# Beginning the linear attention's preparation earlier in a fused attention, expert and linear-attention kernel

## The chip, the core and the metric

The kernel runs on one core of one Trainium2 chip. The time is device microseconds of that core, the median of repeated executions; before the change it is 2023.33 us (three runs, 2021.16 to 2025.43). The core has TensorE (PE: matrix products and transposes), VectorE (DVE), ScalarE (ACT), GpSimd (POOL) and SyncE (SP, which issues most transfers). Each engine takes its own instructions strictly in the order in which the program writes them, and waits on semaphores for the others. "PEld" in the profile is TensorE's loading of weights.

## What is computed

Four layers on x of 4 batches x 1024 tokens x 128 features, all in float32, each with a layer norm before and a residual sum after:

```python
x = L0_attn_a_x
x = x + _L0_attn_a_ref(_layernorm(x, axis=-1), ...)   # causal softmax attention, 16 heads of 64
x = x + _L0_ffn_ref(_layernorm(x, axis=-1), ...)      # 32 experts, the best 2 for each token
x = x + _L0_attn_b_ref(_layernorm(x, axis=-1), ...)   # gated linear attention, 16 heads of 8
x = x + _L0_ffn_ref(_layernorm(x, axis=-1), ...)      # the same experts again
```

The linear attention is causal over the tokens of a batch and works on features of the projections:

```python
qf = softplus(q) * (g + 1e-6);  kf = softplus(k)          # g = sigmoid(x @ Wg.T + bg)
kv_cum = cumsum(kf[..., :, None] * v[..., None, :], axis=2);  z_cum = cumsum(kf, axis=2)
out = einsum('bhtd,bhtde->bhte', qf, kv_cum) / (einsum('bhtd,bhtd->bht', qf, z_cum) + 1e-6)[..., None]
out = out.transpose(0, 2, 1, 3).reshape(B, T, h * dh) @ Wo.T
```

## The kernel before

x stays in on-chip memory throughout, as 32 tiles of 128 tokens x 128 features (`x_sb`); batch b has the tiles 8b to 8b+7. The order of the instructions is written out by hand: helpers are generators, and each `next()` puts one more piece of a helper into the program. What is named "turn" or "slot" below is a place in this written order, not a time.

**Attention** (lines 477 to 834). For each batch and each of 8 pairs of heads, `project` computes qT and kT (the pieces pk and pq) and the values va (two pieces pv of 8 records each in the profile), and eight `slot`s work on one block of 128 rows each: scores `s` (L588), maxima `nmx` (L597), exponentials `p`, sums, transposes `pt` (L677) and the weighted values `po` (L694). The pieces of the next pair are put between the slots. For the very first pair all six pieces of `project(0, 0)` stand ahead of the first slot. Every second pair, `project_out` adds the output projection `pw` (L709) to x (L714 on DVE). For the batches 0 to 2 the experts run beside the next batch's attention by sorting (`experts`: scatter to memory, 128-row products, and 16 gathering transfers L439 that POOL issues and that add into x). What of batch 2's gathers isn't issued when attention ends stands in `queue` and is issued later.

After the last slot, `project_out` for the last pairs of batch 3 is written as a loop over 8 tiles, with the layer-norm statistics of four tiles after each fourth (`statistics`, L122 to L127, whose `rstd_mf` comes from POOL). Then SP loads all 32 expert matrices, `we_sb`, in four parts (L844) into memory that held, among other things, `wo_sb`.

**Dense experts for batch 3** ("f", lines 1115 to 1145). The last eight tiles are two groups of four (`qs`). `routed` makes the weights of the experts for a group: normalized x (`xn_f`, L873, DVE), transposes and copy (`xnT_f`, L885, ACT), router logits `pl_f` (L892), softmax (`ex_f`, L905, ACT), the best two (`w_f`, L925, DVE). `dense` then takes a pair of tiles at a time, in eight steps g of four experts: one product `pe_f` of 128x512 for each tile (L956; five PSUM banks), whose four quarters are weighted and summed. In five of the steps DVE does this straight into x (L978, 8 instructions); in the steps 1, 4 and 6 ACT writes the weighted quarters to buffers `t_f` (L966) and POOL sums them: L972 for two buffers, then the halvings L990 and L991. This sum, the tile's share, is added to x by DVE (L937) in `settle`: two pairs later at the first step of a pair, and for the last two pairs by `settle(0)`, at the end of `dense`.

Beside the dense experts stand the first two preparations of the linear attention, `prepare(0)` and `prepare(1)`, each for four tiles of batch 0: statistics (L1024, L1025 on DVE, a chain of four small operations L1030 to L1033 on POOL), normalized x (`xn_l`, L1039, ACT), transposes and copy (`xnT_l`), four projections `pj` (L1057) with four copies each on ACT, exponential, sigmoid and logarithm on ACT, `y` (L1079, DVE), four sums on POOL (L1086, L1087) and a product on DVE (L1092). The pieces are placed by two rules. While the first `routed` is written, each of its 15 pieces is followed by one piece of `prepare(0)`. Then `fill(turn)` runs in each of 64 turns of `dense`: one piece of one preparation, each fourth turn one entry of `queue`, and in turn 56 the product `products(0)`, that is `kv(0)` (L1100, POOL).

**Linear attention** (lines 1147 to 1248). For each of the 32 tiles u: PE adds `kv(u)` into running sums in PSUM (`cum`, L1162), POOL makes `kv(u+1)`, DVE multiplies the sums with q (`m`, L1182), PE adds the rest that the next tile needs (`carry`, L1170, which has to wait for `m`), DVE finishes (`num`, L1191, and three small operations), and later pieces transpose, project and add to x. `ahead` puts pieces of the preparations 2 to 7 between these. The sums of a POOL product and those of the dense experts stand in one queue, POOL's.

**The experts again** ("s", lines 1250 to 1272): batch 0 by sorting, beside the dense form for the batches 1 to 3, with 18 buffers of the pool `mps`.

The names that the steps below use: `project` and the loop over `pairs` (L721 to L824), the `project_out` loop (L830), `routed` (L851), `dense` and `settle` (L928 to L995), `prepare` (L1018), `products` (L1095), `fill` (L1122), and the loop over u (L1228).

Of the kernel before, what the change touches and what calls it, by code (L numbers as in the profile page):

```python
# [8 lines left out]
F32 = mybir.dt.float32  # L9
U32 = mybir.dt.uint32  # L10
AF = mybir.ActivationFunctionType
# [4 lines left out]
P = 128  # L16
# [4 lines left out]
def hybrid_kernel(  # L21
# [450 lines left out]
        nc.sync.dma_start(out=out_v[b], in_=x_sb[:, c0 : c0 + NB, :])  # L472


    sides, queue = [], []
    banks = [None]
    with attn as ph:

        ph.enter_context(tc.manual_schedule())
# [240 lines left out]
        EARLY = (1, 5)  # L720
        for _ in normed(0):  # L721
            pass
        cur, ahead = project(0, 0)
        for _ in ahead:
            pass
        units = []
        weighing = []
        outs, norms = iter(()), iter(())
# [66 lines left out]
        for i, (b, pr) in enumerate(pairs):  # L795
            nm = f"{b}_{pr}"
            qT, kT, va = cur
            oT = otp.tile([P, N], F32, tag="oT", name=f"oT_{nm}")
            oTs.append(oT)
            ahead = iter(())  # L800
            if pr == NPAIR - 3 and b + 1 < B:
                norms = normed(b + 1)
            if i + 1 < len(pairs):
                nxt, ahead = project(*pairs[i + 1])
            twos = {}
            for k, ib in enumerate(ORDER):
# [12 lines left out]
                slot(u, (nm, ib - 1, twos[two], va, oT), k)  # L819
            if i + 1 < len(pairs):  # L820
                cur = nxt
            if pr % HALF == HALF - 1:
                pend = (b, range(pr + 1 - HALF, pr + 1), oTs)
                oTs = []  # L824
# [6 lines left out]
        for c, _ in enumerate(project_out(*pend)):  # L831
            if c % 4 == 3:
                c0 = (B - 1) * NB + c - 3
                known.append(statistics(c0, 4, f"mf_{c0 // 4}"))

    tc.no_sync_barrier()

# [90 lines left out]
    def dense(nm_, qs, store, pool, mp, ps_e, known, beside):  # L928
# [16 lines left out]
        for i, q in enumerate(qs):  # L945
# [46 lines left out]
                    due.append((x_sb[:, q * 4 + c, :], s, q * 4 if c == 3 else None))  # L992
            for _ in nxt:
                pass
        settle(0)  # L995

    lin = ExitStack()
    lw = lin.enter_context(tc.tile_pool(name="lw", bufs=1, reuse_waits="tile"))
    lb = lin.enter_context(tc.tile_pool(name="lb", bufs=3, reuse_waits="tile"))
    lp = lin.enter_context(tc.tile_pool(name="lp", bufs=3, reuse_waits="tile"))
    G = 4
    NE = LD + 1
    PARTS = 3
    EP = NE // PARTS

    tri, eps = mtri, epsn[:, :G]
# [4 lines left out]
    feats = {}  # L1016

    def prepare(t, pool):  # L1018

        c0 = t * G  # L1020
        st = small.tile([P, G, nc.vector.BN_STATS_DIM], F32, tag="stl", bufs=2, name=f"st_l{t}")
        mv = small.tile([P, G, nc.vector.BN_AGGR_DIM], F32, tag="mvl", bufs=2, name=f"mv_l{t}")
        for c in range(G):
            nc.vector.bn_stats(st[:, c, :], x_sb[:, c0 + c, :])  # L1024
            nc.vector.bn_aggr(mv[:, c, :], st[:, c, :])  # L1025
            if c == 1:
                yield
        rstd = small.tile([P, G], F32, tag="rstdl", bufs=2, name=f"rstd_l{t}")
        nb = small.tile([P, G], F32, tag="nbl", bufs=2, name=f"nb_l{t}")
        nc.gpsimd.tensor_tensor(rstd, mv[:, :, 1], eps, ALU.add)  # L1030
        nc.gpsimd.tensor_tensor(rstd, rstd, mhalf[:, :G], ALU.pow)
        nc.gpsimd.tensor_tensor(nb, mv[:, :, 0], rstd, ALU.mult)
        nc.gpsimd.tensor_scalar(nb, nb, -1.0, None, ALU.mult)  # L1033
        yield
        yield
        xn = lb.tile([P, G, D], F32, tag="xn", bufs=2, name=f"xn_l{t}")
        xnT = lb.tile([P, G * P], F32, tag="xnT", bufs=2, name=f"xnT_l{t}")
        for c in range(G):
            nc.scalar.activation(  # L1039
                xn[:, c, :], x_sb[:, c0 + c, :], AF.Identity,  # L1040
                scale=rstd[:, c : c + 1], bias=nb[:, c : c + 1],
            )
        yield
        pt = pool.tile([P, 512], F32, tag="ps1", name=f"pxn_l{t}")
        for c in range(G):
            nc.tensor.transpose(pt[:, c * P : (c + 1) * P], xn[:, c, :], ident)
        nc.scalar.copy(xnT, pt)
        yield
        kq = lb.tile([P, G, 2 * P], F32, tag="kq", name=f"kq_{t}")
        y = lb.tile([P, G, 2 * P], F32, tag="y", bufs=2, name=f"y_{t}")  # L1050
        u = lb.tile([P, G, 2 * P], F32, tag="u", bufs=2, name=f"u_{t}")
        ln = lb.tile([P, G, 2 * P], F32, tag="ln", bufs=2, name=f"ln_{t}")
        gt = lb.tile([P, G, P], F32, tag="gt", bufs=2, name=f"gt_{t}")
        va = lb.tile([P, G, P], F32, tag="va", name=f"va_{t}")
        for c in range(G):
            pj = pool.tile([P, 512], F32, tag="ps1", name=f"pj_{t}_{c}")
            nc.tensor.matmul(  # L1057
                pj, xnT[:, c * P : (c + 1) * P], wc.rearrange("p w d -> p (w d)"),
                start=True, stop=True,
            )  # L1060
            nc.scalar.activation(y[:, c, :], pj[:, : 2 * P], AF.Abs)
            nc.scalar.activation(kq[:, c, :], pj[:, : 2 * P], AF.Relu)
            nc.scalar.copy(gt[:, c, :], pj[:, 2 * P : 3 * P])
            nc.scalar.copy(va[:, c, :], pj[:, 3 * P :])
            if c == G - 1:
                nc.gpsimd.tensor_tensor(
                    gt, gt, bg_sb.unsqueeze(1).to_broadcast([P, G, P]), ALU.add
                )
            yield


        nc.scalar.activation(y, y, AF.Exp, scale=-1.0)
        nc.scalar.activation(u, y, AF.Copy, bias=1.0)
        yield
        yield
        nc.scalar.activation(gt, gt, AF.Sigmoid)
        yield
        yield
        nc.vector.scalar_tensor_tensor(y, u, 1.0, y, ALU.subtract, ALU.subtract)  # L1079
        nc.scalar.activation(ln, u, AF.Ln)  # L1080
        yield
        yield
        yield
        for i in range(2):
            cols = slice(i * P, (i + 1) * P)
            nc.gpsimd.tensor_tensor(ln[:, :, cols], ln[:, :, cols], y[:, :, cols], ALU.subtract)  # L1086
            nc.gpsimd.tensor_tensor(kq[:, :, cols], kq[:, :, cols], ln[:, :, cols], ALU.add)  # L1087
            yield
        yield
        yield  # L1090
        q = kq[:, :, P:]
        nc.vector.scalar_tensor_tensor(q, gt, 1e-6, q, ALU.add, ALU.mult)  # L1092
        feats[t] = (kq, va)

    def products(u):  # L1095

# [16 lines left out]
                sides.remove(e)  # L1113

    with ExitStack() as ph:
        mp = ph.enter_context(tc.tile_pool(name="mpf", bufs=12, reuse_waits="tile"))
        ps_f = ph.enter_context(tc.tile_pool(name="ps_f", bufs=3, space=PSUM, reuse_waits="tile"))
        ps_e = ph.enter_context(tc.tile_pool(name="ps_ef", bufs=5, space=PSUM, reuse_waits="tile"))
        banks[0] = ps_f
        preps = [prepare(t, ps_f) for t in range(2)]  # L1120

        def fill(turn):  # L1122

            if turn == 56:
                for p in preps:
                    for _ in p:
                        pass
                feats["kv"] = products(0)
            next(preps[turn % 2], None)
            if turn % 4 == 3:  # L1130
                if queue:
                    queue.pop(0)()
                on()

        qs = list(range(NT // 4 - 2, NT // 4))
        for _ in routed(qs[0], f"f_{qs[0]}", ps_f, known[0]):
            next(preps[0], None)
        dense("f", qs, False, ps_f, mp, ps_e, known, fill)
        for p in preps:
            for _ in p:  # L1140
                pass
        while sides or queue:
            if queue:
                queue.pop(0)()
            on()

    with lin as ph:
# [80 lines left out]
        for u in range(NT + 4):  # L1228
# [9 lines left out]
            if u < NT:  # L1238
# [24 lines left out]
    with ExitStack() as ph:  # L1263
# [41 lines left out]
```

## Time and profile before

| | |
|---|---|
| median of three runs | 2023.33 us |
| the profiled execution | 2022.32 us |
| its span, first to last instruction | 2020.6 us |
| busy PE, DVE, ACT, POOL | 1887.1, 1500.4, 1228.5, 1136.2 us |
| attention, to the last output projection | 0 to about 1474 us |
| output projection, first router weights | 1474 to 1503 us |
| dense experts of batch 3 | 1503 to 1572 us |
| change to linear attention | 1572 to 1592 us |
| linear attention | 1592 to 1777 us |
| the experts again | 1777 to 2021 us |

A line of the timeline has start, length, engine, line of the program, operation, result and operands, and in brackets how long the engine had stood idle before and what ended that. A line with "x2" merges two instructions that follow each other. A product in float32 with 128x512 results shows as two records. Shares of busy time over the whole span say little here, since the stages have different limits; the busy time by stage and the waits in it say more.

### The profile page before, as it was taken

Reading aid. Unit: us, or ns where it says so; the run is one execution under the profiler, and the core shown is the slowest. Engines: PE = TensorE matmul, PEld = TensorE weight load, DVE = VectorE, ACT = ScalarE, POOL = GpSimd, SP = SyncE. Lnnn points to the kernel's source line nnn. Section 1 sums busy time; section 2 is a strip of 40 time slices with the busy share of each in tenths; the row PEclk is TensorE's granted clock in tenths of the full one; section 3 lists DMA queues with packets and bytes.
Section 4 is the critical chain, followed back from the end, with each engine's and each line's share of the span. In section 5 each row is a group of like instructions: output and inputs, shape, how many; then the busy total and the mean of one; then the engine's idle time right before and its main releaser. Section 6 shows DMA issues by size and latency. Waiting matters only on the chain.

```text
span 2020.6 us, 33597 instructions
## 1 busy us (share of the span) xinstructions
PE 1887.1 (93%) x10066; PEld 1052.0 (52%) x10066; DVE 1500.4 (74%) x4467; ACT 1228.5 (61%) x3889; POOL 1136.2 (56%) x2080
## 2 busy tenths in 40 slices
PE   6999999999999999999999999999979788888897
PEld 3555555555555655555565555555643344543453
DVE  5776776776787676778867776776748778978877
ACT  4766666766667566766766676676645466344433
POOL 3444444454666466556834954665438666537737
PEclk9999999999999999999999999999989899988999
DMA  7000000000002310000132100003311000000251
GB/s 215 1 1 1 1 1 1 1 1 1 1 12 79 108 21 12 1 1 1 45 107 57 21 1 1 1 13 93 101 45 13 6 0 1 0 1 12 62 147 47
DMA packets 111875, 62.54 MB, mean 31 GB/s; under 512 B 5552, under 2 KB 110160, under 8 KB 111568
## 3 DMA queue, kind: packets, MB, share of 16 engines
q1 hardware_dynamic: 101936, 50.43, 8.8%
q0 software_dynamic: 9472, 8.40, 2.1%
q8 instruction: 82, 1.34, 0.3%
q10 hardware_dynamic: 288, 1.57, 0.2%
q14 instruction: 97, 0.79, 0.1%
HBM read 35.60 MB, written 24.77 MB: 30 GB/s over the span
## 4 chain that ended last, share of the span: by engine, by line
PE 63%; DVE 17%; ACT 10%; POOL 7%; issue 3%; DMA 1%; SPq 0%; ACTq 0%; POOLq 0%; DVEq 0%
PE s L588 19%; PE po L694 10%; PE pt L677 10%; DVE nmx L597 5%; PE pe_s L956 4%; ACT p L622 4%; PE pw L709 3%; PE pk L537 3%; DVE x_sb L978 3%; ACT pT L681 2%; PE pe L417 2%; PE pv L551 2%; ACT p L627 1%; PE cum L1162 1%; PE cum L1170 1%
## 5 line engine op out<-in xcount | busy, mean ns | idle before, releaser
L597 DVE TENSOR_REDUCE nmx<-s 128x2 f32<-128x1024 f32 x512 | 604.5, 1220 | 214.5 <-PE s L588 206.2
L622 ACT ACTIVATE p<-s,nmx 128x512 f32<-128x512 f32 (+3 forms) x640 | 360.8, 575 | 309.6 <-DVE nmx L597 277.5
L588 PE MATMUL s<-kT,qT 64*128 64x512 f32 x2048 | 517.8, 619 | 7.8 <-ACT p L622 4.5
L664 POOL TENSOR_SCALAR p<-p,f,ri 128x512 f32<-128x512 f32 (+3 forms) x768 | 502.5, 670 | 0.9 <-issue 0.6
L677 PEld LDWEIGHTS pt<-ident,p 128*128 128x128 f32 x2304 | 250.0, 141 | 218.0 <-issue 90.4
L677 PE MATMUL pt<-ident,p 128*128 128x128 f32 x2304 | 336.0, 282 | 23.4 <-POOL rs L642 7.1
L681 ACT COPY pT<-pt 128x512 f32<-128x512 f32 (+3 forms) x768 | 324.1, 509 | 14.8 <-PE pt L677 10.4
L646 POOL TENSOR_TENSOR rs<-rs,f 128x2 f32<-128x2 f32 x256 | 51.8, 202 | 437.2 <-ACT f L613 407.7
L694 PE MATMUL po<-pT,va 128*64 128x256 f32 (+1 forms) x2560 | 291.1, 365 | 0.6 <-DVE oT L701 0.6
L588 PEld LDWEIGHTS s<-kT,qT 64*128 64x128 f32 x2048 | 173.1, 185 | 195.2 <-issue 95.0
L627 ACT ACTIVATE p<-s,nmx 128x128 f32<-128x128 f32 x512 | 180.3, 365 | 107.5 <-DVE nmx L597 104.8
L694 PEld LDWEIGHTS po<-pT,va 128*64 128x64 f32 x2560 | 167.0, 136 | 97.2 <-issue 32.6
L956 PE MATMUL pe_s<-we_sb,xnT_s 128*128 128x512 f32 x384 | 184.9, 630 | 9.2 <-ACT t_s L966 5.5
L978 DVE SCALAR_TENSOR_TENSOR x_sb<-pe_s,w_s,x_sb 128x128 f32<-128x128 f32 x480 | 129.8, 341 | 32.7 <-PE pe_s L956 31.3
L635 DVE SCALAR_TENSOR_TENSOR p<-p,qtri 128x128 f32<-128x128 f32 x512 | 145.3, 311 | 7.0 <-ACT p L627 3.7
L642 POOL TENSOR_TENSOR rs<-rs 128x2 f32<-128x2 f32 x192 | 43.8, 228 | 187.4 <-DVE ri L655 187.4
L622 ACT ACTIVATION_READ_ACCUMULATOR p<-s,nmx 128x1 f32 x640 | 138.9, 217 | 0.0
L956 PEld LDWEIGHTS pe_s<-we_sb,xnT_s 128*128 128x128 f32 x384 | 74.0, 202 | 100.2 <-issue 58.4
L966 ACT ACTIVATE t_s<-pe_s,w_s 128x128 f32<-128x128 f32 x288 | 78.4, 380 | 50.2 <-PE pe_s L956 47.1
L714 DVE TENSOR_TENSOR x_sb<-pw,x_sb 128x128 f32<-128x128 f32 x128 | 36.9, 289 | 79.5 <-PE pw L709 79.1
L972 POOL TENSOR_TENSOR t_s<-t_s,t_s 128x512 f32<-128x512 f32 x48 | 60.2, 1272 | 60.8 <-ACT t_s L966 60.1
L709 PE MATMUL pw<-wo_sb,oT 128*128 128x128 f32 x512 | 84.5, 290 | 1.8 <-DVE x_sb L714 1.0
(302 smaller groups left out, 2677.0 us busy)
## 6 DMA issues: line engine op xcount, KB each, us to landing
xs<-xs_d SPq DMA_DIRECT2D x33, 256.0 KB, 3.0
ys_d<-ys SPq DMA_DIRECT2D x33, 256.0 KB, 2.4
we<-_ffn_expert_weights_dram SPq DMA_DIRECT2D x24, 256.0 KB, 3.8
xs_d<-zero SPq DMA_DIRECT2D x2, 3008.0 KB, 18.4
we<-_ffn_expert_weights_dram SPq DMA_DIRECT2D x45, 64.0 KB, 1.8
xs_s<-xs_d SPq DMA_DIRECT2D x11, 256.0 KB, 3.7
ys_d<-ys_s SPq DMA_DIRECT2D x11, 256.0 KB, 2.8
we_sb<-_ffn_expert_weights_dram SPq DMA_DIRECT2D x4, 512.0 KB, 6.1
```

Source lines behind the costliest of these rows:

```text
L588: nc.tensor.matmul(st[:, h, :], self.qT[rows, self.ib * P : (self.ib + 1) * P], self.kT[rows, j * 512 : (j + 1) * 512], start=True, stop=True,
L597: nc.vector.tensor_reduce(self.nmx[:, i, :], self.s[i], AX.X, ALU.max, negate=True)
L622: nc.scalar.activation(self.p[h][:, at : at + m * P], self.s[i][:, h, : m * P], AF.Exp, bias=bias, accum_out=self.rs[:, i, h : h + 1],)
L627: nc.scalar.activation(self.p[h][:, at + m * P : at + (m + 1) * P], self.s[i][:, h, m * P : (m + 1) * P], AF.Exp, bias=bias,)
L635: nc.vector.scalar_tensor_tensor(d, d, 1.0, qtri, ALU.mult, ALU.mult, accum_out=self.rs[:, 2, h : h + 1])
L664: nc.gpsimd.tensor_scalar(w, w, self.f[:, i, h : h + 1], self.ri[:, h : h + 1], ALU.mult, ALU.mult,)
L677: nc.tensor.transpose(pt[:, c * P : (c + 1) * P], self.p[h][:, (g + c) * P : (g + c + 1) * P], ident,)
L681: nc.scalar.copy(self.pTs[h][:, g : g + m, self.col : self.col + P], pt[:, : m * P].rearrange("p (c i) -> p c i", c=m),)
L694: nc.tensor.matmul(po[h * DH : (h + 1) * DH, c0:256], va[:, jb, h, :], pTs[h][:, jb, c0:], start=(jb == 0), stop=(jb == n - 1),)
L709: nc.tensor.matmul(pw[:, :P], oTs[i][:, c * P : (c + 1) * P], wo_sb[:, pr, :], start=(i == 0), stop=(i == len(prs) - 1),)
L956: nc.tensor.matmul(pe, xnT[:, c * P : (c + 1) * P], we_sb[:, 4 * g : 4 * g + 4, :].rearrange("p e d -> p (e d)"), start=True, stop=True,)
L978: nc.vector.scalar_tensor_tensor(xs, pe[:, e * D : (e + 1) * D], w[:, c, 4 * g + e : 4 * g + e + 1], xs, ALU.mult, ALU.add,)
```

## The change

- The first two preparations begin in the loop of the last output projection: after the tiles 0, 1, 2 one piece of `prepare(0)` each, after 4, 5, 6 one of `prepare(1)`. That covers the statistics and POOL's four operations; the third piece of each is empty.
- While the first `routed` is written, only eight of its pieces are followed by one of `prepare(0)`: `xn_l` at its first, the transposes at the fifth, the projections only after the router's logits have been written.
- In `fill`, `queue` is served each third turn and `products(0)` comes in turn 46.
- `dense` no longer ends with `settle(0)` but returns `settle`. For batch 3 it is called in the linear attention, after tile u = 1's `finish` has begun; for the last stage at once. For this the buffers `mpf` are reserved outside the linear attention's and kept through it, and these lie 24 KB further up in each partition.
- Of `project(0, 0)` four pieces (kT and qT) stand ahead of the first slot; the two pv pieces come one after each of the first two slots.

The body of `prepare` is moved up unchanged, with a small class `Bank` that hands it the pool of the moment.

```diff
+    class Bank:
+        def tile(self, *a, **k):
+            return banks[0].tile(*a, **k)
+
+    preps = [prepare(t, Bank()) for t in range(2)]
...
-        cur, ahead = project(0, 0)
-        for _ in ahead:
-            pass
+        cur, rest_ = project(0, 0)
+        for _ in range(4):
+            next(rest_)
...
                 slot(u, (nm, ib - 1, twos[two], va, oT), k)
+                next(rest_, None)
...
                 known.append(statistics(c0, 4, f"mf_{c0 // 4}"))
+            elif c < 7:
+                next(preps[c // 4])
...
-        settle(0)
+        return settle
...
+    shares = ExitStack()
+    mpf = shares.enter_context(tc.tile_pool(name="mpf", bufs=12, reuse_waits="tile"))
...
-        preps = [prepare(t, ps_f) for t in range(2)]
...
-            if turn == 56:
+            if turn == 46:
...
-            if turn % 4 == 3:
+            if turn % 3 == 2:
                 if queue:
                     queue.pop(0)()
...
-        for _ in routed(qs[0], f"f_{qs[0]}", ps_f, known[0]):
-            next(preps[0], None)
-        dense("f", qs, False, ps_f, mp, ps_e, known, fill)
+        for i, _ in enumerate(routed(qs[0], f"f_{qs[0]}", ps_f, known[0])):
+            if i in (0, 4, 8, 9, 10, 11, 12, 13):
+                next(preps[0])
+        settle = dense("f", qs, False, ps_f, mpf, ps_e, known, fill)
...
             ahead(3 * u + 2)
+            if u == 1:
+                settle(0)
...
+    shares.close()
...
-        dense("s", qs, True, ps_s, mp, ps_e, [None] * len(qs), pieces)
+        dense("s", qs, True, ps_s, mp, ps_e, [None] * len(qs), pieces)(0)
```

More of the change, by code (lines that the diff above doesn't have):

```diff
@@ L472, in experts, with prepare @@
         nc.sync.dma_start(out=out_v[b], in_=x_sb[:, c0 : c0 + NB, :])
+    G = 4
+    tri, eps = mtri, epsn[:, :G]
+    feats = {}
+    def prepare(t, pool):
+        c0 = t * G
+        st = small.tile([P, G, nc.vector.BN_STATS_DIM], F32, tag="stl", bufs=2, name=f"st_l{t}")
+        mv = small.tile([P, G, nc.vector.BN_AGGR_DIM], F32, tag="mvl", bufs=2, name=f"mv_l{t}")
+        for c in range(G):
+            nc.vector.bn_stats(st[:, c, :], x_sb[:, c0 + c, :])
+            nc.vector.bn_aggr(mv[:, c, :], st[:, c, :])
+            if c == 1:
+                yield
+        rstd = small.tile([P, G], F32, tag="rstdl", bufs=2, name=f"rstd_l{t}")
+        nb = small.tile([P, G], F32, tag="nbl", bufs=2, name=f"nb_l{t}")
+        nc.gpsimd.tensor_tensor(rstd, mv[:, :, 1], eps, ALU.add)
+        nc.gpsimd.tensor_tensor(rstd, rstd, mhalf[:, :G], ALU.pow)
+        nc.gpsimd.tensor_tensor(nb, mv[:, :, 0], rstd, ALU.mult)
+        nc.gpsimd.tensor_scalar(nb, nb, -1.0, None, ALU.mult)
+        yield
+        yield
+        xn = lb.tile([P, G, D], F32, tag="xn", bufs=2, name=f"xn_l{t}")
+        xnT = lb.tile([P, G * P], F32, tag="xnT", bufs=2, name=f"xnT_l{t}")
+        for c in range(G):
+            nc.scalar.activation(
+                xn[:, c, :], x_sb[:, c0 + c, :], AF.Identity,
+                scale=rstd[:, c : c + 1], bias=nb[:, c : c + 1],
+            )
+        yield
+        pt = pool.tile([P, 512], F32, tag="ps1", name=f"pxn_l{t}")
+        for c in range(G):
+            nc.tensor.transpose(pt[:, c * P : (c + 1) * P], xn[:, c, :], ident)
+        nc.scalar.copy(xnT, pt)
+        yield
+        kq = lb.tile([P, G, 2 * P], F32, tag="kq", name=f"kq_{t}")
+        y = lb.tile([P, G, 2 * P], F32, tag="y", bufs=2, name=f"y_{t}")
+        u = lb.tile([P, G, 2 * P], F32, tag="u", bufs=2, name=f"u_{t}")
+        ln = lb.tile([P, G, 2 * P], F32, tag="ln", bufs=2, name=f"ln_{t}")
+        gt = lb.tile([P, G, P], F32, tag="gt", bufs=2, name=f"gt_{t}")
+        va = lb.tile([P, G, P], F32, tag="va", name=f"va_{t}")
+        for c in range(G):
+            pj = pool.tile([P, 512], F32, tag="ps1", name=f"pj_{t}_{c}")
+            nc.tensor.matmul(
+                pj, xnT[:, c * P : (c + 1) * P], wc.rearrange("p w d -> p (w d)"),
+                start=True, stop=True,
+            )
+            nc.scalar.activation(y[:, c, :], pj[:, : 2 * P], AF.Abs)
+            nc.scalar.activation(kq[:, c, :], pj[:, : 2 * P], AF.Relu)
+            nc.scalar.copy(gt[:, c, :], pj[:, 2 * P : 3 * P])
+            nc.scalar.copy(va[:, c, :], pj[:, 3 * P :])
+            if c == G - 1:
+                nc.gpsimd.tensor_tensor(
+                    gt, gt, bg_sb.unsqueeze(1).to_broadcast([P, G, P]), ALU.add
+                )
+            yield
+        nc.scalar.activation(y, y, AF.Exp, scale=-1.0)
+        nc.scalar.activation(u, y, AF.Copy, bias=1.0)
+        yield
+        yield
+        nc.scalar.activation(gt, gt, AF.Sigmoid)
+        yield
+        yield
+        nc.vector.scalar_tensor_tensor(y, u, 1.0, y, ALU.subtract, ALU.subtract)
+        nc.scalar.activation(ln, u, AF.Ln)
+        yield
+        yield
+        yield
+        for i in range(2):
+            cols = slice(i * P, (i + 1) * P)
+            nc.gpsimd.tensor_tensor(ln[:, :, cols], ln[:, :, cols], y[:, :, cols], ALU.subtract)
+            nc.gpsimd.tensor_tensor(kq[:, :, cols], kq[:, :, cols], ln[:, :, cols], ALU.add)
+            yield
+        yield
+        yield
+        q = kq[:, :, P:]
+        nc.vector.scalar_tensor_tensor(q, gt, 1e-6, q, ALU.add, ALU.mult)
+        feats[t] = (kq, va)
@@ L1005, in hybrid_kernel @@
     lp = lin.enter_context(tc.tile_pool(name="lp", bufs=3, reuse_waits="tile"))
-    G = 4
     NE = LD + 1
@@ L1009, in hybrid_kernel @@
     EP = NE // PARTS
-    tri, eps = mtri, epsn[:, :G]
     wc = lw.tile([P, 4, P], F32, name="wc")
@@ L1014, in hybrid_kernel @@
         nc.vector.tensor_copy(wc[:, i, :], wT[wn])
[L1016 to L1093, printed above, removed]
@@ L1115, in hybrid_kernel @@
     with ExitStack() as ph:
-        mp = ph.enter_context(tc.tile_pool(name="mpf", bufs=12, reuse_waits="tile"))
         ps_f = ph.enter_context(tc.tile_pool(name="ps_f", bufs=3, space=PSUM, reuse_waits="tile"))
```

## The prediction

> **What bounds the kernel now.** I read the page first, then the busy time by stage, then the chain of waits, then the timeline of the two places where the stages say that TensorE (PE) stands still. The span is 2020.6 us and the profiled execution took 2022.32 us, so 1.7 us lie around the span; the median of the runs is 2023.33 us, 1.0 us above that execution. All sums below are differences made inside the profiled execution; I put them on the median at the end. 0.2% is 4 us, about what a measurement of this kernel can tell from no change.
>
> PE is busy 93% of the span, so only the places where it isn't can give time:
>
> ```profile
> 1474.00:1495.00 21.00, 12.89 (x61) 8.24 (x58) 9.02 (x44) 5.57 (x18) 3.74 (x6) 0.76 0.38 100
> 1495.00:1528.00 33.00, 25.59 (x65) 11.71 (x64) 26.61 (x90) 22.56 (x63) 21.73 (x21) 0.88 0.07 9
> 1528.00:1572.00 44.00, 41.60 (x90) 17.18 (x88) 36.15 (x131) 25.33 (x77) 37.33 (x33) 0.94 0.11 14
> 1572.00:1592.00 20.00, 8.98 (x14) 4.54 (x15) 13.21 (x19) 1.03 (x3) 16.21 (x17) 0.66 0.05 7
> ```
>
> The columns are window and length, then busy time of PE, weight loads, VectorE (DVE), ScalarE (ACT), GpSimd (POOL), then granted clock. PE idles 8 of 21 us at the end of attention, 7 of 33 at the start of the dense experts, and 11 of 20 where these give way to linear attention. POOL is 85% and 81% busy in the last two rows. The timeline of the last window says why:
>
> ```profile
> 1571.63 5.68 DVE L937 TENSOR_TENSOR x_sb<-x_sb,t_f 128x128 f32<-128x128 f32 x2
> 1571.85 3.02 POOL L972 TENSOR_TENSOR t_f<-t_f,t_f 128x512 f32<-128x512 f32 x2
> 1574.29 2.65 POOL L1100 TENSOR_TENSOR kv<-kq,va 128x1024 f32<-128x1024 f32 x1
> 1577.00 4.21 PE L1162 MATMUL cum<-kv,mtri 128*128 128x384 f32 x6 [7.23 <-POOL kv L1100]
> 1582.52 0.79 DVE L937 TENSOR_TENSOR x_sb<-x_sb,t_f 128x128 f32<-128x128 f32 x1 [5.21 <-POOL t_f L991]
> 1583.65 2.12 POOL L1100 TENSOR_TENSOR kv<-kq,va 128x1024 f32<-128x1024 f32 x1
> 1587.23 4.21 PE L1170 MATMUL cum<-kv,rest 128*128 128x384 f32 x6 [6.02 <-DVE m L1182]
> 1591.23 2.26 PE L1162 MATMUL cum<-kv,mtri 128*128 128x384 f32 x6
> ```
>
> Each row is start, length, instruction, and in brackets the wait before it. PE waits 7.2 us for the first product kv(0), which stands in POOL's queue behind the experts' sums, and 6.0 us for m(0) on DVE, which stands behind the four last shares (L937); these wait for POOL's L991. And at the head of the dense stage:
>
> ```profile
> 1486.72 1.65 ACT L1039 ACTIVATE xn_l<-x_sb,nb_l,rstd_l 128x128 f32<-128x128 f32 x4 [17.42 <-POOL nb_l L1033]
> 1488.27 0.56 ACT L885 COPY xnT_f<-pxn_f 128x512 f32<-128x512 f32 x1
> 1498.60 0.29 ACT L905 ACTIVATE ex_f<-ex_f 128x128 f32<-128x128 f32 x1
> 1504.29 2.08 PE L956 MATMUL pe_f<-we_sb,xnT_f 128*128 128x512 f32 x2 [4.37 <-ACT t_f L966]
> 1516.64 3.04 POOL L972 TENSOR_TENSOR t_f<-t_f,t_f 128x512 f32<-128x512 f32 x2
> ```
>
> The router's copy xnT_f waits on ACT behind xn_l, which waits for POOL; its logits then stand on PE behind three projections pj, its exponential on ACT behind all four and two long passes.
>
> **The change part by part.**
>
> *First pair.* The two pv groups (16 matmuls, 1.78 us in the chain of waits at 20.79) leave the place ahead of the first scores: -1.8. They return between score groups; the second and third score groups start after about 0.9 us of pv, and the third finds DVE free. I take -1.0; ends 0 (all given back) and -1.8.
>
> *Statistics beside the out-projection.* Eight pairs of L1024/L1025 at 0.40 us join DVE: +3.2, of which the waits before L714 (1.1 in all, of them some 0.9 in reach) hide 0.9, and wc and xn_f come 2.1-2.3 later (1484.1 for 1482.0). Without this cover it would be the whole 3.2. POOL's two chains of four (1.9 us each, as 1484.79 to 1486.69) run where POOL is idle; the router's rstd_mf stand behind them but are wanted later. SP's loads of we_sb, which wait for PE's last read of wo_sb, leave about 1 us later; landing takes a median of 6.1, so the first is there by 1488, before its use at 1493. xn_l of both groups no longer waits for POOL.
>
> *Router first.* xn_f ends at 1485.3; transposes and copy (0.73 and 0.56) give 1486.5; the logits start at 1486.7, their maximum at 1488.2, the difference ends at 1488.9. The exponential stands behind two projections on ACT: PE starts them at 1488.0, the first result comes 2.1 later (as 1489.57 to 1491.68), two sets at 0.99 end at 1492.4; with 0.3 for ex_f and 2.7 for the DVE steps to w_f (3.66 before, less L1079, which moves on) the weights are there at 1495.4 instead of 1502.6: 7.2 earlier.
>
> *What this runs into.* ACT then owes two sets (2.0), exponential and copy (2.2), table and sigmoid (1.9) before xn_l(1), to 1498.6; PE has xn_l(1)'s transposes ahead of the third expert group and stands about 3 us, to 1500.8 (2.2 after xn_l begins, as 1486.72 to 1488.9). Then three groups, two pj and one set of transposes at 0.86 a tile: 1508.8. With 1.1 for four multiplications on ACT, POOL's first L972 starts at 1510.0 instead of 1516.64: 6.6 earlier.
>
> *POOL's queue.* From there POOL has no gap. Before, it needed 67.0 us from the first L972 to kv(1) (1516.64 to 1583.65), with 3.8 idle (before 1537.10) and 13 transfers, as many as remain in the new order; prepare(0)'s two ln/kq pairs, 2.6 each, were before it and come into it: 67.0 - 3.8 + 5.2 = 68.4. So kv(1) runs 1578.4 to 1580.5. Popping the 15 transfers each third turn instead of each fourth changes none of the sum; where two follow each other the pitch is 1.87 (1529.88 to 1531.75), before a sum it is 1.1. The tail holds 16 L972, 13 transfers, four sets of halvings, gt, four ln/kq pairs and kv(0). Short end, undisturbed rows: 16 x 1.25 + 9 x 1.1 + 4 x 1.87 + 4 x 2.9 + 1.3 + 4 x 2.58 + 2.12 = 62.7. Long end, the dearest rows: 16 x 1.6 + 13 x 2.3 + 4 x 3.2 + 1.3 + 4 x 2.8 + 2.65 = 83.5. settle(2) of the fourth pair needs L991 of the second, some 38 us into the tail (1548); DVE comes there about 1553 (1560.5 less 7 to 8): no wait.
>
> *Transition.* kv(0) now stands four sums and eight halvings ahead of kv(1), at about 1564 to 1567; cum(0), m(0) and carry(0) are done by about 1573, since DVE owes no share first. The next wait is PE's cum(1) for kv(1): start 1580.6 for 1591.23. PE has then stood about 7 us, so I price the six at 4.21 (after 7.2 us of waiting) and not at 2.26: num(1) begins 5.0 after cum(1) (4.21, the last third of m at 0.56, and the hand-over), at 1585.6, instead of 1594.12. Gain 8.5.
>
> The Trainium skill ("TensorE: Matmul & The Clock Gate", What's actually happening) says that about 3.4 us of idleness halve PE's clock and as much steady work restores it; the trace agrees (4.21 against 2.26). By a warm PE the gain here would be 10.5.
>
> *Shares at u = 1.* Four L937, 0.24 each where POOL does not read (the pair at 1560.47 took 0.48) to 2.84 each (5.68 a pair): 1.0 to 11.4 on DVE, behind them m(2) and PE's carry(2). POOL's queue after kv(1) is prepare(2)'s chain, kv(2), kv(3), to about 1586.8, then a wait for ACT's gt (9.4 us before); the shares come at 1587.5. I take 1.0, beside the 1.1 that m(2) waits for PE in the trace: 0.
>
> The Trainium skill ("SBUF — State Buffer", SBUF: two separate sides) speaks against this move: a DVE operation with two SBUF inputs and a POOL operation that reads SBUF exclude each other for their whole length. The trace agrees (5.68 beside L972 and kv). By that rule, if the shares met kv(2) and kv(3), they would lose up to 4.2 and the sum would be about -6.
>
> *Memory.* The share buffers stay allocated through linear attention. No new copy or transfer follows, and the last stage's tiles lie on memory freed earlier: 0, between -0.3 and +0.3 (all that L937 waited there).
>
> Sum: -1.0 - 8.5 + 0 = -9.5: 2012.8 by the profiled execution, 2013.8 on the median. I say **2014**.
>
> **Rivals.**
> *POOL pays contended prices:* halfway to the long end, 75 us. DVE with 82% in that stage speaks for it, the 67.0 measured under the same mixture against. kv(1) ends at 1587.1, the gain is 1.0 + 8.5 - 6.6 = 2.9: 2020.4, no measurable change. The change would not do what it says: the product moved, its successor didn't.
> *Slower:* POOL's tail at its long end. With no idle left, each contended L972 and each transfer behind another delays kv(1) in full, and all later products with it: 83.5 us give 1595.6, 15.1 late: 2013.8 + 15.1 = 2028.9. It decides from a tail of 78 us. For it: L937 and L972 stretch each other in the trace; against: DVE is out of dense work from about 1564 (1571.6 less the 7 to 8 won at its head).
> *Shares meet products:* should the four shares come while kv(2) and kv(3) run, DVE waits for both, 2 x 2.12, less the 1.1 it has in hand: 3.1 later, 2017. The margin is 0.7 us (1586.8 to 1587.5), and a POOL queue that runs late moves both alike. This is the rule of the Trainium skill named above as a case of its own.
> *More:* POOL at its short end, because DVE is idle in its last 16 us: 5.6 earlier, 2008.
>
> **How the numbers follow.** Forecast 0.46, shares meet products 0.08, more 0.20, contended prices 0.12, long end 0.14: faster 0.74, same 0.12, slower 0.14. The range runs from 2006 (short end, first pair at -1.8) to 2024 (tail about 78); the forecast's own is 2010 to 2018.
>
> **What would show it.** Right: w_f near 1495; xnT_f's copy without xn_l's wait; PE's wait before cum(0) gone as a wait for L972's queue, a wait before cum(1) for kv in its place; no L937 before m(0), four short ones after finish(1). Wrong: the first L972 not before 1516 (ACT's queue decides), L937 near 2.8 us in linear attention, or linear attention itself longer than before, since the sum carries the shift to the end unchanged.

## The result, and the profile after

The changed kernel takes 2011.62 us, the median of six runs (2008.61 to 2014.35), beside 2023.5 us for the kernel before (six runs, 2021.16 to 2025.43): a ratio of 0.9942, with a 95% interval of 0.993 to 0.9954, that is 9 to 14 us less. The forecast was 2014 with 2006 to 2024.

The profiled execution of the changed kernel took 2013.61 us, with a span of 2011.9, 8.7 less than before. It is not quite like for like: the last output projection of attention begins at 1476.06 us after and at 1474.27 before. That wanders by itself: in an experiment below whose attention is the program of before it begins at 1477.84. So I count the stages from there ("from attention's end"), and read no difference of a few tenths in one profile. A second scatter lies behind it: the kernels with early preparations have the same program from attention's end to POOL's first expert sum, but for some transfers in four of them, and need 34.4 us for it in six profiles and 36.0 to 36.3 in five, the changed kernel's among these. With it goes the last step of `w_f`, which takes 0.70 to 0.76 us in the six and 1.15 to 1.34 in the five. Times from attention's end to anything later can differ by this, some 1.7 us.

Busy time by stage, changed kernel (columns as before the change: window and length, busy PE, weight loads, DVE, ACT, POOL, granted clock, DMA share, GB/s):

```profile
1476.00:1497.00 21.00, 15.61 (x62) 10.20 (x60) 12.45 (x69) 6.88 (x24) 5.54 (x11) 0.76 0.39 100
1497.00:1530.00 33.00, 26.81 (x68) 11.90 (x67) 24.87 (x80) 28.54 (x68) 21.61 (x17) 0.93 0.09 11
1530.00:1574.00 44.00, 37.62 (x81) 15.89 (x79) 31.50 (x106) 16.68 (x62) 41.21 (x35) 0.90 0.13 16
1574.00:1586.00 12.00, 8.83 (x23) 4.28 (x22) 8.28 (x25) 2.91 (x11) 11.60 (x14) 0.90 0.00 0
```

The change to linear attention is over after 12 us instead of 20, and PE stands for 3 of them instead of 11. But POOL is now busy 94% of the dense experts' second half and 97% of the transition, and PE, which had 41.6 busy in the 44 us before, has 37.6. The timeline of these stages:

```profile
1549.89 0.69 DVE L553 SCALAR_TENSOR_TENSOR kq<-gt,kq 128x512 f32<-128x512 f32 x1 [6.16 <-POOL kq L548]
1552.54 15.81 PE L1049 MATMUL pe_f<-we_sb,xnT_f 128*128 128x512 f32 x32 [5.59 <-DVE x_sb L1071]
1568.17 2.64 POOL L1114 TENSOR_TENSOR kv<-kq,va 128x1024 f32<-128x1024 f32 x1
1575.23 2.10 PE L1176 MATMUL cum<-kv,mtri 128*128 128x384 f32 x6
1578.07 1.45 DVE L1196 TENSOR_TENSOR m<-cum,kq 128x384 f32<-128x384 f32 x3
1580.53 2.12 POOL L1114 TENSOR_TENSOR kv<-kq,va 128x1024 f32<-128x1024 f32 x1
1582.71 3.40 PE L1176 MATMUL cum<-kv,mtri 128*128 128x384 f32 x6 [1.86 <-POOL kv L1114]
1586.74 1.36 DVE L1205 TENSOR_REDUCE num<-m 128x144 f32<-128x1152 f32 x1
1588.86 0.87 DVE L1030 TENSOR_TENSOR x_sb<-x_sb,t_f 128x128 f32<-128x128 f32 x4
```

The waits for kv(0) (7.23 us) and for m(0) behind the shares (6.02) are gone; what remains is 1.86 us before cum(1), for kv(1) on POOL. The four shares stand after num(1) and cost 0.87 together. New, and not in the forecast, are the first two rows: DVE stands 6.16 us before its last product of `prepare(1)` and PE 5.59 behind it.

The head of the dense stage:

```profile
1485.69 1.11 DVE L966 TENSOR_SCALAR xn_f<-x_sb,mv_mf,rstd_mf 128x128 f32<-128x128 f32 x4
1487.37 0.58 ACT L978 COPY xnT_f<-pxn_f 128x512 f32<-128x512 f32 x1 [4.76 <-PE pxn_f L977]
1494.38 0.34 ACT L998 ACTIVATE ex_f<-ex_f 128x128 f32<-128x128 f32 x1
1497.12 1.20 DVE L1018 TENSOR_TENSOR w_f<-rwx,w_f 128x128 f32<-128x128 f32 x1
1512.12 2.49 POOL L1065 TENSOR_TENSOR t_f<-t_f,t_f 128x512 f32<-128x512 f32 x2 [10.21 <-ACT t_f L1059]
```

xnT_f waits for PE alone and no longer for xn_l; the weights are ready at 1498.3 instead of 1502.6, the first POOL sum starts at 1512.12 instead of 1516.64. Counted from attention's end it is 6.3 us earlier.

### The profile page after: what moved, and what is told of

Its sections match the earlier page's. It is cut to its first block, busy times and chain, and to the rows that moved or that the text cites. A ratio compares the mean times of both kernels' runs of the same rounds, so it can differ in the third digit from the quotient of the medians.

```text
span 2011.9 us, 33593 instructions
## 1 busy us (share of the span) xinstructions
PE 1887.9 (94%) x10066; PEld 1054.3 (52%) x10066; DVE 1492.5 (74%) x4467; ACT 1228.4 (61%) x3889; POOL 1136.8 (57%) x2080
## 3 DMA queue, kind: packets, MB, share of 16 engines
q8 instruction: 82, 1.34, 0.3%
## 4 chain that ended last, share of the span: by engine, by line
PE 62%; DVE 15%; ACT 9%; POOL 9%; issue 4%; DMA 1%; SPq 0%; ACTq 0%; POOLq 0%; DVEq 0%
PE s L678 19%; PE po L784 10%; PE pt L767 10%; DVE nmx L687 5%; PE pe_s L1049 4%; ACT p L712 3%; PE pw L799 3%; PE pk L627 3%; DVE x_sb L1071 2%; POOL x_sb L439 2%; ACT pT L771 2%; PE cum L1184 2%; PE cum L1176 2%; PE pe L417 2%; PE pv L641 1%
## 5 line engine op out<-in xcount | busy, mean ns | idle before, releaser
L1065 POOL TENSOR_TENSOR t_s<-t_s,t_s 128x512 f32<-128x512 f32 x48 | 60.2, 1274 | 59.2 <-ACT t_s L1059 58.7
```

## The experiments

The theory (POOL): between the first expert sum (L1065, before L972) and kv(1) POOL never rests, so the linear attention begins when POOL's queue has passed kv(1), plus what stands between kv(1) and num(1). The first rival (SHARES): only the shares ahead of m(0) held it. The second (HEAD): the earlier begin of the dense experts pays by itself, since PE is busy 93%. All runs go by one table, which the text then reads; the first three columns of numbers are us from one profile each (the first of them with the scatter of 1.7 us named above), the ratio is to the kernel before on the same chip, with its 95% interval. The runs stand on several chips, so that ratios compare more closely than medians.

| kernel | attention's end to kv(1) | kv(1) to num(1) | num(1) to num(31) | median | ratio |
|---|---|---|---|---|---|
| before | 109.4 | 10.5 | 175.7 | 2023.3 to 2024.8 | 1 |
| changed | 104.5 | 6.2 | 175.5 | 2011.62 | 0.9942 [0.993, 0.9954] |
| shares alone | 109.5 | 5.0 | 177.0 | 2019.63 | 0.9978 [0.9969, 0.9987] |
| preparations alone | 104.2 | 10.9 | 177.0 | 2019.68 | 0.9981 [0.9972, 0.999] |
| all but shares | 101.9 | 10.6 | 176.0 | 2016.38 | 0.997 [0.9958, 0.9982] |
| all but first pair | 104.5 | 5.0 | 176.4 | 2010.57 | 0.9937 [0.9923, 0.995] |
| first product at 56 | 104.4 | 6.2 | 175.5 | 2014.12 | 0.9944 [0.993, 0.9957] |
| queue each 4th turn | 105.8 | 6.6 | 174.0 | 2011.88 | 0.9944 [0.9931, 0.9958] |
| DVE product later | 102.5 | 7.0 | 175.6 | 2012.27 | 0.9943 [0.9929, 0.9956] |
| transfers split | 91.5 | 5.0 | 182.7 | 2005.97 | 0.9908 [0.9893, 0.9923] |
| split, DVE later | 88.9 | 5.0 | 183.7 | 2006.78 | 0.9912 [0.9899, 0.9926] |
| transfers all early | 90.2 | 5.0 | 176.2 | 1998.91 | 0.9879 [0.9864, 0.9894] |
| all early, DVE later | 89.0 | 5.0 | 177.0 | 1999.61 | 0.9884 [0.9869, 0.9899] |

### Taking the change apart

Shares alone: the kernel before, with `settle` called in the linear attention as in the change, its buffers kept through it, and nothing else.

```diff
-        settle(0)
+        return settle
...
             ahead(3 * u + 2)
+            if u == 1:
+                settle(0)
```

> The kernel before, with only the four last shares moved behind u = 1 of the linear attention. Theory POOL (the change to linear attention waits for POOL's queue, up to kv(1)): kv(1) stays where it was, at 1585.8 of the profile before; cum(0) at 1577.0 to 1581.2, m(0) and carry(0) right behind, cum(1) at about 1586 and num(1) near 1589 instead of 1594.1: about 5 us less than before, 2018.5. Rival SHARES (the shares ahead of m(0) were all that held the linear attention): 10 us less, 2013.5. Rival HEAD (the earlier begin of the dense experts is what pays): no change, 2023.5.

Preparations alone: the changed kernel with everything but the early preparations undone.

```diff
-        for _ in range(4):
-            next(rest_)
+        for _ in rest_:
+            pass
...
-            if turn == 46:
+            if turn == 56:
...
-            if turn % 3 == 2:
+            if turn % 4 == 3:
...
         settle = dense("f", qs, False, ps_f, mpf, ps_e, known, fill)
+        settle(0)
...
-            if u == 1:
-                settle(0)
```

> Only the early preparations: statistics beside the out-projection and the router ahead of the projections; the shares at the end of the dense experts, kv(0) in turn 56, the queue each fourth turn, the first pair's pv as before. Theory POOL: POOL's first L972 comes about 4.5 us earlier and so does kv(1), but m(0) waits for the shares and these for POOL's last halving: num(1) near 1591, 3 to 4 us less than before, 2020. Rival SHARES: no change, 2023.5. Rival HEAD: the 7 us won at the head arrive, 2015 or less.

All but the shares: only the last two hunks of that diff.

> The changed kernel with the four last shares back at the end of the dense experts, all else as changed. Theory POOL: kv(1) as in the changed kernel (1580.5 to 1582.6), but the shares wait for the last halving at 1580.6, m(0) comes near 1584, carry(0) behind it and num(1) near 1591: about 4.5 us more than the changed kernel, 2016. Rival SHARES: 10 us more, 2021.5. Rival HEAD: no change against the changed kernel, 2011.6.

All but the first pair: only its first hunk.

> The changed kernel with all six pieces of the first projection ahead of the first scores again. As predicted: 1.0 us more than the changed kernel, 2012.6. Rival (all of it is given back behind the first scores, as the profile of the changed kernel has it, whose attention ends no earlier): no change, 2011.6.

The shares alone give 2019.63, the preparations alone 2019.68, everything but the shares 2016.38. Neither SHARES (2013.5, and 2023.5 without them) nor HEAD (2015 at most from the preparations alone) holds; POOL was within 1.2 us in all three. The table says how the change pays in two parts: kv(1) comes 4.9 us earlier (109.4 to 104.5), and num(1) follows it after 6.2 instead of 10.5. The first part is there in the kernels with early preparations, the second in those with the shares out of the way. Without the second, the timeline of the kernel with all but the shares shows what is lost:

```profile
1577.94 2.12 POOL L1114 TENSOR_TENSOR kv<-kq,va 128x1024 f32<-128x1024 f32 x1
1578.02 2.19 DVE L1030 TENSOR_TENSOR x_sb<-x_sb,t_f 128x128 f32<-128x128 f32 x1 [0.42 <-POOL t_f L1084]
1580.94 1.45 DVE L1197 TENSOR_TENSOR m<-cum,kq 128x384 f32<-128x384 f32 x3
1581.52 4.21 PE L1185 MATMUL cum<-kv,rest 128*128 128x384 f32 x6 [6.83 <-DVE m L1197]
1585.52 2.36 PE L1177 MATMUL cum<-kv,mtri 128*128 128x384 f32 x6
```

kv(1) is done at 1580.1, but carry(0) waits for m(0), which waits for the last share, which waits for POOL's halving and then takes 2.19 us beside kv(1), where such an addition alone takes 0.2. And without the first part, in the kernel with the shares alone:

```profile
1580.79 3.89 PE L1163 MATMUL cum<-kv,mtri 128*128 128x384 f32 x6 [7.23 <-POOL kv L1102]
1584.52 2.10 PE L1171 MATMUL cum<-kv,rest 128*128 128x384 f32 x6
1587.38 2.12 POOL L1102 TENSOR_TENSOR kv<-kq,va 128x1024 f32<-128x1024 f32 x1
1589.56 2.20 PE L1163 MATMUL cum<-kv,mtri 128*128 128x384 f32 x6 [2.94 <-POOL kv L1102]
```

the 7.23 us before kv(0) are unchanged, and kv(1) ends last instead of the shares. The linear attention starts after the later of two chains, and both begin in POOL's queue.

Undoing the first pair costs nothing that the runs can tell (2010.57 against 2011.62). The trace says why. PE's scores at the start, of the kernel with the first pair undone and then of the changed kernel:

```profile
21.19 1.02 PE L633 MATMUL pq<-xnT_a,wq_sb 128*128 128x512 f32 x2
22.05 1.95 PE L641 MATMUL pv<-wkv_sb,xnT_a 128*128 128x128 f32 x16
23.93 1.99 PE L678 MATMUL s<-kT,qT 64*128 64x512 f32 x8
39.56 1.99 PE L678 MATMUL s<-kT,qT 64*128 64x512 f32 x8
```

```profile
20.91 1.02 PE L633 MATMUL pq<-xnT_a,wq_sb 128*128 128x512 f32 x2
22.62 1.99 PE L678 MATMUL s<-kT,qT 64*128 64x512 f32 x8 [0.69 <-ACT qT L636]
25.50 1.05 PE L641 MATMUL pv<-wkv_sb,xnT_a 128*128 128x128 f32 x8
39.05 1.99 PE L678 MATMUL s<-kT,qT 64*128 64x512 f32 x8
```

From the end of the last projection, the first scores come 0.7 instead of 1.7 us later; by the scores near 39 us it is 17.12 instead of 17.35. So 1.0 us comes out at the first scores and not 1.8, since these now wait for qT on ACT, and 0.2 of it is left.

### The order within POOL's queue

The first product back at turn 56, and, in another kernel, the queue served each fourth turn again. The loop over `preps` at turn 46 finds nothing left to do, since the last pieces of the two preparations come at the turns 18 and 35; so only kv(0) moves in the first of these kernels:

```diff
-            if turn == 46:
+            if turn == 56:
```

> The changed kernel with one thing undone: the last steps of both preparations and the first product kv(0) are put back at turn 56 of the dense stage, from turn 46. Theory POOL (the linear attention begins when POOL's queue has passed kv(1), whatever stands in what order ahead of it): the work ahead of kv(1) is the same, kv(0) only comes closer to it; kv(1) stays at about 1580.5, cum(1) then follows cum(0), m(0) and carry(0) about 3 us later than in the changed kernel at most, and finds PE warm: 2011.6 to 2013.5. Rival ORDER (kv(0) moved ahead is what pays, since PE no longer stands waiting for the first product): the wait before cum(0) comes back at some 7 us and cum(1) with it: 2016 to 2018.

```diff
-            if turn % 3 == 2:
+            if turn % 4 == 3:
```

> The changed kernel with the left-over transfers again popped each fourth turn. Theory POOL: between the first sum and kv(1) the same 13 transfers stand, only kv(0) passes some of them, so kv(1) and the end are unchanged: 2010.5 to 2013. Rival (the transfers' place moves the end): 3 us or more on either side.

Ratios of 0.9944 for both, 0.9942 for the changed kernel (the median of 2014.12 was measured beside 2024.81 for the kernel before, which is 1.3 to 1.6 us above its other medians; the runs with the DVE product later and with the transfers split were measured beside it too). In the first, kv(0) starts at 1574.37 instead of 1568.17 and kv(1) is where it was, 104.4 us from attention's end; in the second kv(1) comes 1.3 later in the profile and the linear attention is 1.5 shorter. So undoing either of two of the change's parts, the product moved forward and the transfers moved forward, costs nothing: they exchange places ahead of kv(1) in a queue whose sum stays within about 1 us (68.4 and 69.5 us from the first expert sum to kv(1), and 68.4 in the changed kernel).

One pair of runs limits this. The preparations alone and all but the shares differ by these two parts and the first pair, and by 3.3 us (2019.68 against 2016.38, on one chip); 2.3 of them stand between the first expert sum and kv(1) (69.8 against 67.5). The two intervals just overlap, but with the shares at the end of the dense experts something in that order seems to pay. Which of the three parts it is no run tells.

### PE's new wait

DVE's last product of `prepare(1)` ten of its pieces later, so that DVE no longer stands behind POOL for it. `fill` serves each preparation every second turn, so this is twenty turns (55 instead of 35), and not ten as the expectation says:

```diff
         yield
         yield
+        for _ in range(10 if t == 1 else 0):
+            yield
         q = kq[:, :, P:]
...
             if turn == 46:
-                for p in preps:
-                    for _ in p:
-                        pass
+                for _ in preps[0]:
+                    pass
                 feats["kv"] = products(0)
```

> The changed kernel with DVE's last product of the second preparation (kq by the gate) moved ten turns back, so that DVE no longer stands 6.2 us behind POOL's sum of kq; PE's wait of 5.59 us in the last expert group, which that caused, should be gone. Theory POOL: kv(1) on POOL's queue ends last anyway, so PE's earlier end buys nothing: 2010.5 to 2012. Rival PE (the dense experts' last matmul sets when the linear attention starts): the 5.6 us come out of the end, 2006.

The wait of 5.59 us is gone and the time is 2012.27, ratio 0.9943: no gain. PE and POOL at the transition:

```profile
1559.54 3.17 PE L1051 MATMUL pe_f<-we_sb,xnT_f 128*128 128x512 f32 x7
1564.97 2.64 POOL L1116 TENSOR_TENSOR kv<-kq,va 128x1024 f32<-128x1024 f32 x1
1567.67 3.85 PE L1177 MATMUL cum<-kv,mtri 128*128 128x384 f32 x6 [4.96 <-POOL kv L1116]
1577.31 2.12 POOL L1116 TENSOR_TENSOR kv<-kq,va 128x1024 f32<-128x1024 f32 x1
1579.48 4.21 PE L1177 MATMUL cum<-kv,mtri 128*128 128x384 f32 x6 [6.03 <-POOL kv L1116]
```

PE is done with the dense experts at 1562.7, 11.4 us earlier than in the changed kernel when both are counted from attention's end (1.7 of that is the scatter ahead of the first sum), and then stands 4.96 and 6.03 us for POOL. PE's end was not the bound.

### The transfers out of POOL's queue

If POOL's queue is the bound, the 13 left-over transfers in it (15 with the two ahead of the first sum) are the work that can leave it. Seven are issued in the first seven turns, where POOL idles for 10 us, the other eight one by one in the linear attention; a second kernel adds the later DVE product.

```diff
-            if turn % 3 == 2:
+            if turn < 7:
...
-        while sides or queue:
-            if queue:
-                queue.pop(0)()
-            on()
...
             if u == 1:
                 settle(0)
+            if u and (sides or queue):
+                if queue:
+                    queue.pop(0)()
+                on()
```

> The changed kernel with the left-over transfers taken out of POOL's queue between the first expert sum and kv(1): seven are issued in the first seven turns, where POOL is idle for 10 us, and the other eight one by one within the linear attention. Theory POOL: the 68.4 us from the first sum to kv(1) lose some 13 transfers at 1.1 to 1.87 us, 14 to 20 us; kv(1) is done before PE's dense end at about 1575, which takes over as the bound with its 5.6 us of waiting for DVE: num(1) at about 1579 to 1581 instead of 1586.7, so 2004 to 2006. Rival PE: PE's dense end bounds already in the changed kernel, so nothing comes of it: 2010 to 2012. Rival LATER: the transfers moved into the linear attention delay its products and give the gain back: 2011 or more, with linear attention over 176 us from num(1) to num(31).

> Both of the two edits before: transfers out of POOL's queue, and DVE's product of the second preparation ten turns back. Theory POOL: with POOL's queue out of the way PE's dense end bounds, so the 5.6 us that PE waited for DVE now count, where alone they did not: 1999 to 2002. Rival PE: the sum of what the two give alone, with no more than 1 us between them. If POOL is still the bound after the transfers are gone: the same as with the transfers out alone.

2005.97 and 2006.78. The first lies in the range of POOL, but not for the reason given there: num(1) came at 1572.57, 14.2 us earlier than in the changed kernel instead of 6 to 8, and the linear attention then took 182.7 us instead of 175.5. So the rival LATER was true in its mechanism, though not in its time (2011 or more). The expected stop at PE's dense end was not there, since PE's wait for DVE fell from 5.59 to 1.00 together with POOL's delay that had caused it. With the later DVE product num(1) comes another 2.6 us earlier from attention's end, but 1.65 of that is the scatter ahead of the first sum (36.0 and 34.4), and 0.9 lies in POOL's tail. The total gains nothing: that expectation, 1999 to 2002, failed. Both rivals of that run fit its time, what the two edits give alone added up (about 2006.6) and the transfers alone (2005.97).

Both losses pointed to the eight transfers in the linear attention. So all 15 of the queue before the first expert sum:

```diff
             elif c < 7:
                 next(preps[c // 4])
+            if c == 0:
+                for _ in range(3):
+                    queue.pop(0)()
...
-            if turn % 3 == 2:
+            if turn < 7:
...
             if i in (0, 4, 8, 9, 10, 11, 12, 13):
                 next(preps[0])
+            if i < 5:
+                queue.pop(0)()
```

> The changed kernel with all 15 left-over transfers issued before POOL's first expert sum: three beside the out-projection, five beside the first router, seven in the first seven turns; none in the linear attention. In the trace POOL is idle there for 8, 10 and 10 us. Theory POOL: as with the transfers split, num(1) at about 1572.6, but the linear attention from num(1) to num(31) is again 175.5 us as in the changed kernel, so the 14 us stay: 1998 to 2001. Rival DRIFT (linear attention gives an early start back by itself, whatever the transfers do, because PE's clock or the preparations hold it): 2005 to 2007, as with the split. Rival HEAD (eight transfers ahead of the gates' sum delay the first POOL sum by 3 us or more and DVE's router steps stretch beside them): 2001 to 2004.

> The kernel with all transfers early and, besides, DVE's product of the second preparation ten turns back. With the split transfers that edit brought num(1) 2.1 us earlier but the total nothing (2006.78 against 2005.97). Theory POOL: without the transfers in the linear attention the 2 us stay: 1 to 2 us below the kernel with all transfers early. Rival: the same time within 1 us, since POOL's kv(1) has become the bound again.

1998.91 us, ratio 0.9879: as expected, 24 us below the kernel before and twice what the change gave. POOL needs 55.8 us from the first sum to kv(1), with the transfers split 55.5; kv(1) is at 90.2 instead of 91.5 us from attention's end by the scatter ahead of that sum, and the linear attention takes 176.2. The waits for POOL's products in the linear attention, first with the transfers split, then with all of them early (waiting instruction, releaser, then us in total, times, longest, from 1572 to 1765 us):

```profile
PE cum L1171 <- POOL kv L1114: 7.3, 4, 2.9
```

```profile
PE cum L1181 <- POOL kv L1117: 0.3, 1, 0.3
```

And the busy time by stage with all of them early:

```profile
1497.00:1530.00 33.00, 28.85 (x77) 12.70 (x76) 25.51 (x98) 30.27 (x77) 26.54 (x22) 1.00 0.14 17
1530.00:1565.00 35.00, 34.00 (x81) 14.81 (x80) 28.67 (x106) 17.54 (x66) 26.83 (x25) 1.00 0.00 1
1565.00:1586.00 21.00, 19.00 (x61) 10.20 (x60) 16.84 (x42) 8.20 (x27) 12.23 (x14) 1.00 0.00 0
```

POOL falls to 77% and waits for ACT seven times between the first sum and kv(1), 11.1 us in all, while PE is busy 34 of 35 us at a granted clock of 1.00. POOL's queue is no longer without gaps, and the dense experts go by PE. That PE alone is now the bound isn't shown, for what ends last ahead of cum(1) is still kv(1), by 0.42 us:

```profile
1567.79 2.13 POOL L1117 TENSOR_TENSOR kv<-kq,va 128x1024 f32<-128x1024 f32 x1
1569.97 2.20 PE L1181 MATMUL cum<-kv,mtri 128*128 128x384 f32 x6 [0.42 <-POOL kv L1117]
```

The later DVE product adds nothing there (1999.61 against 1998.91, intervals that overlap almost wholly), where 1 to 2 us had been expected; the rival, the same time within 1 us, is what came. num(1) came 1.2 earlier, with cum(1) again waiting for kv(1) (0.43), and the linear attention took 0.8 more. Where that 0.8 arises was not followed up. The kernel with all transfers early is the fastest of the study.

## Why the prediction came out

The forecast was 9.5 us less than before; the medians say 11.9, with an interval of 9 to 14.

- **POOL's queue.** The row that carried it, 68.4 us from the first sum to kv(1), was exact: 1512.12 to 1580.53 is 68.4. The mixture of before was the right price, and neither end (62.7, 83.5) came true; this rules out both the contended and the long-end rival here. The runs with other orders of the same work, the early preparations among it, took 67.5 to 69.8 us by the same rows, so the sum was right to about 1 us, and its agreement to a tenth is luck.
- **The head.** The first sum was forecast 6.6 us earlier and came 6.3 earlier from attention's end. The exponential behind two sets, the short stand of PE before xn_l(1) (2.04 us where 3 were forecast) and the later start of `xn_f` behind the statistics (1.9 us where 2.1 were forecast) are in the trace. The weights came 1.1 us later than forecast, mostly because the last step of w_f took 1.20 us instead of 0.29.
- **The transition.** Forecast 8.5, measured 9.2 from attention's end: num(1) 110.7 us after it instead of 119.9. The step that was mis-sized is cum(1) at 4.21 "after about 7 us of standing": PE came from carry(0) and had stood 1.86, and the six took 3.40. carry(0), forecast to be done by about 1573, ended only at 1580.85 (1579.1 if both profiles are counted from attention's end), since PE left the dense experts late, by the wait that is told under "What was missed". The step as it was forecast, 6.03 us of standing and 4.21 for the six, is what the kernel with the DVE product later shows. The wait alone does not set the price of the six: with the shares alone they took 2.20 after 2.94.
- **The first pair.** Mis-sized: -1.0 was taken, 0.2 is what is left. The bound of 0 was named as one end, and the row nearest to it (the third score group "finds DVE free") was only argued. The lower end of the range, 2006, does not follow from the terms named for it: 2013.8 less 5.6 and 0.8 is 2007.4.
- **Shares at u = 1.** 0 was forecast and seen (1.0 for the four, 0.87 measured), but narrowly: they began at 1588.86, 0.13 us after kv(3) had ended, where a margin of 0.7 was forecast, and only because the slow cum(1) had held num(1) back. In the four kernels without split transfers in which num(1) follows kv(1) after 5.0 us they met the end of kv(3) and took 1.82 or 1.83. With the transfers split they took 3.72, beside a kv of 2.61, and m(2) came about 1 us later than with all transfers early. In no run did they meet two products, so the rival's 3.1 was not tested. The Trainium skill ("SBUF — State Buffer", SBUF: two separate sides) says that a DVE operation with two SBUF inputs and a POOL operation that reads SBUF exclude each other for a whole instruction; these rows agree, and so does w_f's step of 1.20, which began at 1497.12 and ended 0.15 after POOL's addition of 1496.90 to 1498.17.
- **What was missed.** The forecast looked for a DVE that waits for POOL only in `settle(2)`, and found none there. The wait came at the last product of `prepare(1)`: 6.16 us on DVE, 5.59 on PE. Three pieces of this preparation have gone into the loop of the output projection, so its product comes in turn 35 instead of 41, ahead of DVE's expert sums there, while POOL, which now has the sums of `prepare(0)` in its tail too, is not done with kq. Turn 46 has no part in it: with the first product at turn 56 the two waits are 6.16 and 5.58. The kernel before has the same wait on DVE with 2.57 us (before 1553.66), and the forecast did not price it. "DVE is out of dense work from about 1564" was wrong with it: its last expert sums end at 1577.3. It cost nothing only because POOL's kv(1) was later still, as the run without that wait shows. The forecast thus rested on the right chain, and an error of 11 us on another chain stayed without effect.
- **The rest.** Transition, first pair and linear attention (175.7 to 175.5) make 9.6 us. The last stage took 249.7 instead of 250.8 in these two profiles and 249.8 to 253.9 in others with the same program there, so the remaining 2.3 us between that sum and the medians stay unexplained; they are within the interval.

## What to carry to other kernels

Where an in-order queue without gaps ended last, moving one instruction forward within it paid nothing, and neither did freeing the engines beside it. Take work out of such a queue, into a stretch where that engine idles, and look at both sides of the move: the same eight transfers that cost nothing beside the output projection and the router cost 6 to 7 us within the linear attention. Price the start of a stage as the later of all chains that feed it: here either chain shortened alone gave about a third of the gain (3.9 and 3.8 of 11.9 us), and only both together the whole. And where a helper is begun earlier, all its later pieces move forward with it: ask which other engine takes part in them, and what that engine must now wait for ahead of its own work.

## What the runs showed of the hardware

A gathering transfer costs POOL more than its own slot. POOL's rows in the changed kernel, and then the same operation without a transfer ahead of it, in the kernel with the transfers split:

```profile
1527.24 1.55 POOL L439 DMA_INDIRECT x_sb<-ys_d,row  x1 [0.16 <-issue]
1528.33 1.23 POOL L1083 TENSOR_TENSOR t_f<-t_f 128x256 f32<-128x256 f32 x1
1529.64 0.46 POOL L1084 TENSOR_TENSOR t_f<-t_f 128x128 f32<-128x128 f32 x1
```

```profile
1524.69 0.72 POOL L1083 TENSOR_TENSOR t_f<-t_f 128x256 f32<-128x256 f32 x1
1525.49 1.03 POOL L1084 TENSOR_TENSOR t_f<-t_f 128x128 f32<-128x128 f32 x1
```

The halving starts 1.1 us after the transfer and the next operation 1.31 after the halving instead of 0.80: 0.5 more. (The starts are what to compare. The 1.03 of the last row stands beside a product on DVE, 1525.53 to 1526.20.) The same 0.5 stands on kv behind a transfer (2.64 for 2.12) and on the expert sums (3.00 for 2.49 a pair). So by these rows a transfer in a full queue is worth about 1.6 us, and 13 of them some 21. The queue gave only 13 when they left, since it then had to wait for ACT again: 11.1 us with all transfers early, 3.02 the longest. The two together make 24, somewhat more than the rows say.

PE's speed at the start of a run is not the same each time: the first two records of the pq products took between 1.02 and 1.92 us among the 13 profiles, though each of these gives a granted clock of 1.00 for that stretch, and the second pair ended between 20.75 and 22.28. Where it ended late, attention mostly ended late too; the cause was not looked for.
